# Second part's constants made beside the experts, zeros stored by ScalarE, first tiles planned first, last pair routed in three parts

## The chip, the cores and the metric

One core of one Trainium2 chip runs the whole program. The metric is the device time of one execution in microseconds (us). Three runs of the kernel before took 3497.92, 3501.64 and 3504.68 us, so the median is 3501.64 us.

## The reference, cut to what matters

The reference is a two-layer network over 16 sequences of 569 rows (441 image tokens and 128 text rows) of 256 numbers:

```python
h = tokenizer(x)                       # conv, one attention over the 441 tokens
h = concatenate([h, txt])              # 569 rows
h = h + window_attention(layernorm(h)) # 64-row windows
# experts: each row goes to the two best of 8, by gate probability
probs = softmax(layernorm(h) @ gate_w + gate_b)
top2_vals, top2_idx = top_k(probs, 2)
h = h + sum over the two experts e of
        probs[e] * (gelu(xf @ W1[e] + b1[e]) @ W2[e] + b2[e])
h = h + phasor_attention(layernorm(h))
h = h + lstm_layer(layernorm(h))       # 569 steps, hidden size 256, and sums over time
```

The change touches the seam between the window attention with its routing (the first part) and the experts, and the constants that only the phasor attention and the LSTM (the second part proper) need.

## The kernel before, in words

**First part (to L919).** The sequences are taken in 8 pairs. Each pair has 9 chunks of 128 rows. Nine streams of work (`features`, `norms`, `routing`, `texts`, `projections`, four slots of `windows`, two of `tokens`) are generators that announce their next instruction's engine and an estimate of its time. `Order.run` (L220) merges them into one written order by a list schedule, so PE, DVE, ACT and POOL run exactly the order that the planner wrote. SP, which only issues DMAs, is ordered by the framework's own scheduler. Inside a pair, `norms` and `windows` go through the chunks in the order `CHUNKS` = 7, 0, 1, 2, 3, 4, 5, 6, 8 (L362). Chunk 7 holds text only; chunks 6 and 8 need the last token unit. A finished window stores its rows in `HD` (L761) and hands them to `sent_rows`, which writes the normalised rows into `XN`.

**Routing (L767 to L891).** For each entry of `PARTS` (L364) the gate's logits, the softmax, the top two, and the rows' places in the experts' regions are computed. `place0` is the running first free place of each of the 8 experts; each part adds its counts to it (L864), so the parts form a chain. `send` then scatters each chunk's rows into `XS` in HBM by two indirect DMAs that POOL issues (L883), each followed by a small memset (L889). Pairs 0 to 6 are one part each; pair 7 has two: chunks 0 to 4 and chunks 5 to 8.

**Constants of the second part (L932 to L1027).** Between the two parts, in program order, stand the loads of `W_hh`, `lin`, `lstm_b`, `lb`, `W_ih`, `Wk1` and their like (ACT and SP issue them), DVE's work on `lin`, `lstm_b` and the bias pieces, POOL's memsets of `begins` and the four `X` buffers, and POOL's scalings of `W_hh` (L1006, six) and `W_ih` (L1013, two). The framework's scheduler mixes them with the end of the routing.

**Experts (L1035 to L1179).** `experts` turns the 8 counts into a table `where` for 79 tiles of 256 rows: which expert a tile belongs to and where its rows begin. The last tile of each expert can reach past its rows, so zeros are stored behind each expert's last row (L1112, eight stores of 256 KB issued by SP, each with an address that SP loads from `where` first). The rows' stores by `send` and the zeros are declared independent. SP issues four weight loads `w` (L1100, 1154 KB each), then the eight zero stores, then the row loads `xs` (L1106), which need everything in `XS` to have landed. The buffers of `w` lie where `XN` lay, so the first `w` load waits until the last `send` has landed. A tile is: transpose (L1140), copy (L1145), 8 matmuls (L1153), gelu (L1160), 8 matmuls (L1167), bias (L1173), store (L1174). Four slots interleave, and there are five buffers of `w` and `xs`.

Of the kernel before, what the change touches and what calls it, by code (L numbers as in the profile page):

```python
# [282 lines left out]
def kernel(ctx: ExitStack, tc: tile.TileContext, a: dict, out: bass.AP):  # L283
# [80 lines left out]
    PARTS = [(p, 0, NC) for p in range(NP - 1)] + [(NP - 1, 0, 5), (NP - 1, 5, NC)]  # L364
    WINDOWS = 4
    ROWS, XNS = 18, 4
    xns = {}

# [251 lines left out]
    def norms():  # L620

        for n in range(NC * NP):
            p, i = divmod(n, NC)
            c = CHUNKS[i]
            if n >= XNS:
                before = n - XNS
                yield "at", ("turned", before // NC, CHUNKS[before % NC])
            yield "at", ("token", p, min(c, 6)) if c != 7 else ("text", p)
            xn = xns[p, c] = wk.tile([128, D], F32, name=f"wxn{p}_{c}", tag="wxn", bufs=XNS)
            yield from norm(H[p, c], xn, f"w{p}_{c}", "w")  # L630
            first.mark(("columns", p, c))
# [20 lines left out]
    def windows(slot):  # L652

        kb, vb = KB[slot], VB[slot]
        for n in range(slot, NC * NP, WINDOWS):
            p, i = divmod(n, NC)
            c = CHUNKS[i]
# [104 lines left out]
            if n >= WINDOWS:  # L762
                before = n - WINDOWS
                yield "at", ("normed", before // NC, CHUNKS[before % NC])
# [169 lines left out]
    Whh = load_kxn(ls, "W_hh", 2, 4 * D, nc.scalar)  # L934
# [4 lines left out]
    nc.scalar.dma_start(lin, a["W_lin"].rearrange("(k p) n -> p k n", p=128))  # L939
    nc.vector.tensor_tensor(lin[:, :, :1], lin[:, :, 1:], lin[:, :, :1], ALU.subtract)  # L940
    nc.vector.tensor_copy(wl, lin[:, :, :1].to_broadcast([128, 2, 128]))
    shut = ls.tile([128, 1], F32, name="shut")
    nc.vector.tensor_tensor(shut, frow("b_lin", 1), frow("b_lin", 1, 1), ALU.subtract)
    nc.vector.tensor_scalar(shut, shut, 2.0, None, ALU.mult)
# [3 lines left out]
    by_unit = [cols[:, COL[n] : COL[n] + 2] for n in ("fw", "bw")]  # L948
    nc.vector.tensor_tensor(weights[:, 0, :], by_unit[0], by_unit[1], ALU.subtract)
    nc.vector.tensor_scalar(weights[:, 0, :], weights[:, 0, :], 0.5, None, ALU.mult)  # L950
    nc.vector.tensor_scalar(weights[:, 1, :], by_unit[1], -0.5, None, ALU.mult)
    nc.vector.tensor_scalar(weights[:, 2, :], by_unit[1], 0.5, None, ALU.mult)

    begins = {n: ls.tile([128, NB * (n + 1)], F32, name=f"begins{n}") for n in {n for _, _, n in RUNS}}
    for n, t in begins.items():
        nc.gpsimd.memset(t, 1.0)
        nc.gpsimd.memset(t.rearrange("p (b t) -> p b t", b=NB)[:, :, :1], 0.0)
# [6 lines left out]
    for t in XS_OF:  # L964
        nc.gpsimd.memset(t.rearrange("p k t x -> p (k t x)"), 0.0)
    one3 = ls.tile([128, 128], BF16, name="one3")
    nc.vector.memset(one3, 1.0)
# [3 lines left out]
    for t in bias3.values():  # L971
        nc.vector.memset(t, 0.0)
    with tc.tile_pool(name="lb", bufs=1) as lbp:
        lb = lbp.tile([128, 4 * D], F32, name="lb")
        for t, of in ((lstm_b, 0), (lb, 1)):
            nc.scalar.dma_start(t, a["lstm_b"][of].to_broadcast([128, 4 * D]))
        nc.vector.tensor_tensor(lstm_b, lstm_b, lb, ALU.add)
        v = lstm_b.rearrange("p (q r) -> p q r", r=128)[:, :, 64:96]
        nc.vector.tensor_scalar(v, v, 2.0, None, ALU.mult)

        def in_pieces(x, name):

            m = x.shape[0]
            pieces = lbp.tile([m, 3, D], BF16, name=name + "_pieces")
            left = lbp.tile([m, D], F32, name=name + "_left")
# [4 lines left out]
            return pieces  # L990

        for n, t in bias3.items():
            pieces = in_pieces(frow(n)[:1], n)
            for i in range(3):
                for j in range(2):
                    nc.sync.dma_start(t[i : i + 1, j, :], pieces[:, i, :])
# [3 lines left out]
    def gate_columns(w, gate):  # L1000
        return w.rearrange("p (q r) -> p q r", r=128)[:, :, 32 * gate : 32 * gate + 32]

    for k in range(2):
        for gate in (0, 1, 3):
            v = gate_columns(Whh[:, k, :], gate)
            nc.gpsimd.tensor_scalar(v, v, 0.5, None, ALU.mult)  # L1006

    bg = ExitStack()
    l1w = bg.enter_context(tc.tile_pool(name="l1w", bufs=1))
    Wih = load_kxn(l1w, "W_ih", 2, 4 * D)  # L1010
    for v in (Wih[:, 0, :], Wih[:, 1, :]):
        v = gate_columns(v, 2)
        nc.gpsimd.tensor_scalar(v, v, 2.0, None, ALU.mult)  # L1013
    l1 = {}
    for n in ("Wk1", "Wq1", "Wv", "Wo"):
        l1[n] = load_kxn(l1w, n, 2, D)
    for n in ("Wk2", "Wq2"):
        t = l1w.tile([128, 2, 2, 64], F32, name=n)
        for i in range(2):
            nc.sync.dma_start(t[:, :, i, :], a[n].rearrange("(k p) n -> p k n", p=128))  # L1020
        l1[n] = t
    masks = l1w.tile([128, 2, 128], F32, name="masks")
    nc.sync.dma_start(masks, a["masks"].rearrange("p (i n) -> p i n", i=2))
    none = l1w.tile([128, 1], F32, name="none")
    nc.vector.memset(none, 0.0)
    S = [l1w.tile([128, 2, 2, D], F32, name=f"S{p}") for p in range(0, NP, 2)]
    yat = l1w.tile([128, NP, 2, NC], mybir.dt.int32, name="yat")  # L1027
# [7 lines left out]
    def experts(g, mo, slots):  # L1035


        NT, most = TILES[g], E * REGION[g]
        count = tiling.tile([128, E], F32, name=f"count{g}", tag="count", bufs=1)
        nc.vector.tensor_tensor(  # L1040
            count, place0[:, g, :], frow("region", E, g * E), ALU.subtract
        )
        need = tiling.tile([128, E], F32, name=f"need{g}", tag="need", bufs=1)
# [5 lines left out]
        for e in range(E):  # L1049
            nc.vector.tensor_tensor(  # L1050
                end[:, e + 1 : e + 2], end[:, e : e + 1], need[:, e : e + 1], ALU.add
            )
        past = tiling.tile([128, NT, E], F32, name=f"past{g}", tag="past", bufs=1)
        nc.vector.tensor_tensor(
            past, frow("tile_no", NT).unsqueeze(2).to_broadcast([128, NT, E]),
            end[:, 1:].unsqueeze(1).to_broadcast([128, NT, E]), ALU.is_ge,
        )
        expert = tiling.tile([128, NT], F32, name=f"expert{g}", tag="expert", bufs=1)
        nc.vector.tensor_reduce(expert, past, AX.X, ALU.add)
        nc.vector.tensor_tensor(  # L1060
            past, past, need.unsqueeze(1).to_broadcast([128, NT, E]), ALU.mult
        )
        first = tiling.tile([128, NT], F32, name=f"first{g}", tag="first", bufs=1)
        nc.vector.tensor_reduce(first, past, AX.X, ALU.add)
        nc.vector.tensor_tensor(first, frow("tile_no", NT), first, ALU.subtract)
        nc.vector.tensor_scalar(first, first, float(TILE), None, ALU.mult)
        nc.vector.scalar_tensor_tensor(
            first, expert, float(REGION[g]), first, ALU.mult, ALU.add
        )
        where = tiling.tile([128, 2 * NT + E], mybir.dt.int32, name=f"where{g}", tag="where", bufs=1)  # L1070
        nc.vector.tensor_scalar(where[:, :NT], first, float(most), None, ALU.min)
# [867 lines left out]
```

## Time and profile before

| what | us |
|---|---|
| median of three runs | 3501.64 |
| the profiled execution | 3500.74 |
| its span, first to last instruction | 3498.9 |
| PE busy in the span | 3160.7 |
| DVE busy | 1958.2 |
| ACT busy | 1229.8 |
| POOL busy | 767.2 |

The profile is of one execution. The span is cut into 40 slices of 87.5 us; a digit tells how busy an engine was in a slice, in tenths. A windows view gives the busy time of each engine in any stretch, and a timeline lists the instructions of a stretch: start, duration, engine, line, operation, what it writes and reads, and how long the engine sat idle before, with what released it. "SPq" and "ACTq" are the sequencers that issue DMAs; their durations are issue times, not transfers.

### The profile page before, as it was taken

The page shows a single profiled execution, that of the slowest core. Times are in us where ns is not written, and L with a number is a line of the kernel's source. Part 1 is how long each engine was busy: PE and PEld are TensorE (multiplying, and loading weights), DVE is VectorE, ACT ScalarE, POOL GpSimd, SP SyncE. Part 2 cuts the span into 40 slices and gives each one's busy share as a digit, 9 for nine tenths or more (in the row PEclk, how much of TensorE's full clock was granted, in tenths as well). Part 3 has the DMA queues.
Part 4 walks back from the last instruction along what each step waited for, and adds up shares of the span by engine and source line. Part 5 has one row for each costly group of instructions (what it writes and reads, how often), then busy time and mean ns, then how long its engine had stood idle before and what let it go on. Part 6 is the DMA issues. An engine that isn't in the chain of part 4 may idle for free.

```text
span 3498.9 us, 91880 instructions
## 1 busy us (share of the span) xinstructions
PE 3160.7 (90%) x37356; PEld 2388.9 (68%) x37356; DVE 1958.2 (56%) x6420; ACT 1229.8 (35%) x3914; POOL 767.2 (22%) x1343
## 2 busy tenths in 40 slices
PE   6999999899659999996799999999999999999873
PEld 4666666666448888885677777777777777776542
DVE  4677677776621111113466666666676666666444
ACT  3555455544212222222433333333333333322220
POOL 1253455435610000003412111111112221001000
PEclk9999999999779999998999999999999999999996
DMA  4121222101266666662323222232232222231304
GB/s 172 51 68 42 74 82 80 37 22 39 97 229 231 223 230 223 228 215 75 110 63 90 82 85 79 84 86 83 78 86 80 73 77 79 69 107 60 127 29 108
DMA packets 186903, 363.17 MB, mean 104 GB/s; under 512 B 25600, under 2 KB 120880, under 8 KB 173424
## 3 DMA queue, kind: packets, MB, share of 16 engines
q1 hardware_dynamic: 164448, 310.04, 28.1%
q0 software_dynamic: 13824, 37.77, 3.4%
q10 hardware_dynamic: 8208, 9.48, 0.9%
q8 instruction: 295, 4.83, 0.6%
q14 instruction: 128, 1.05, 0.1%
HBM read 238.87 MB, written 118.33 MB: 102 GB/s over the span
## 4 chain that ended last, share of the span: by engine, by line
PE 43%; DVE 5%; ACT 3%; POOL 2%; issue 1%; DMA 1%; DVEq 0%; SPq 0%; ACTq 0%; POOLq 0%
PE g L1637 16%; PE xm_False L1503 7%; PE g L1602 3%; PE eq L1297 2%; PE z L1328 2%; PE ek L1297 2%; PE v L1317 2%; PE po_False L1473 2%; PE ds_False L1378 1%; PE fin L1700 1%; ACT act L1653 1%; DVE ab L1659 1%; PE r_False L1446 1%; ACT th L1678 1%; DVE cT L1672 1%
## 5 line engine op out<-in xcount | busy, mean ns | idle before, releaser
L1637 PE MATMUL g<-W_hh,X 128*16 128x128 f32 (+1 forms) x18176 | 606.6, 274 | 70.0 <-DVE X L1680 68.7
L1637 PEld LDWEIGHTS g<-W_hh,X 128*16 128x16 f32 (+1 forms) x18176 | 454.2, 103 | 242.6 <-DVE X L1680 194.1
L1653 ACT ACTIVATE act<-g 128x96 f32<-128x96 f32 x568 | 142.5, 251 | 658.2 <-PE g L1637 656.8
L1659 DVE SCALAR_TENSOR_TENSOR ab<-act 128x64 f32<-128x64 f32 x568 | 127.7, 225 | 383.9 <-ACT act L1653 379.3
L1167 PE MATMUL y<-w,hT 128*128 128x256 f32 x1264 | 289.9, 382 | 6.3 <-ACT hT L1160 2.5
L1269 POOL DMA_INDIRECT yg<-YS,yat x144 | 147.8, 1026 | 662.5 <-DMA YS<-ys 626.0
L1160 ACT ACTIVATE hT<-hp,w 128x256 f32<-128x256 f32 x316 | 132.5, 472 | 456.2 <-PE hp L1153 293.3
L1153 PE MATMUL hp<-xt,w 128*128 128x256 f32 x1264 | 285.7, 379 | 0.0
L1503 PE MATMUL xm_False<-W_ih,dxT_False 128*128 128x256 f32 x1088 | 282.0, 393 | 1.7 <-ACT dxT_False L1189 1.1
L1167 PEld LDWEIGHTS y<-w,hT 128*128 128x128 f32 x1264 | 236.7, 190 | 46.8 <-ACT hT L1160 16.1
L1153 PEld LDWEIGHTS hp<-xt,w 128*128 128x128 f32 x1264 | 238.8, 190 | 33.9
L1678 ACT ACTIVATE th<-cT 128x32 f32<-128x32 f32 x569 | 130.4, 229 | 371.7 <-DVE toT L1675 367.5
L1173 DVE TENSOR_TENSOR ys<-y,w 128x512 f32<-128x512 f32 x79 | 54.6, 691 | 357.9 <-PE y L1167 357.9
L1602 PE MATMUL g<-xp,ident 128*32 128x128 f32 x4552 | 231.0, 275 | 8.3 <-DMA xp<-XPD 8.3
L1503 PEld LDWEIGHTS xm_False<-W_ih,dxT_False 128*128 128x128 f32 x1088 | 193.4, 190 | 51.2 <-issue 26.6
L1212 POOL TENSOR_SCALAR r_False_rstd<-r_False_mv,cols 128x2 f32<-128x2 f32 x36 | 14.4, 400 | 785.5 <-DVE r_False_mv L1207 785.1
L1680 DVE SCALAR_TENSOR_TENSOR X<-toT,th 128x32 f32<-128x32 f32 x569 | 109.1, 192 | 116.6 <-ACT th L1678 114.8
L883 POOL DMA_INDIRECT XS<-XN,at x144 | 150.5, 1045 | 38.8 <-issue 24.6
L674 PE MATMUL wqk<-wxT,wqkv 128*128 128x128 f32 x1152 | 152.0, 280 | 6.2 <-ACT wxT L668 5.9
L674 PEld LDWEIGHTS wqk<-wxT,wqkv 128*128 128x128 f32 x1152 | 141.6, 194 | 21.8 <-ACT wxT L668 12.2
L1602 PEld LDWEIGHTS g<-xp,ident 128*32 128x32 f32 x4552 | 128.7, 110 | 38.9 <-issue 29.5
L1145 DVE COPY xt<-xtr 128x512 f32<-128x512 f32 x79 | 51.0, 686 | 159.0 <-PE xtr L1140 159.0
(341 smaller groups left out, 6022.0 us busy)
## 6 DMA issues: line engine op xcount, KB each, us to landing
w<-in_wpack SPq DMA_DIRECT2D x79, 1154.0 KB
xp<-XPD SPq DMA_DIRECT2D x71, 512.0 KB
XPD<-xp_False SPq DMA_DIRECT2D x256, 128.0 KB
taps<-in_taps SPq DMA_DIRECT2D x16, 1764.0 KB
xs<-XS SPq DMA_DIRECT2D x79, 256.0 KB
YS<-ys SPq DMA_DIRECT2D x79, 256.0 KB
HD<-h SPq DMA_DIRECT2D x72, 128.0 KB
fh<-HD SPq DMA_DIRECT2D x72, 128.0 KB
```

The source lines that it names most:

```text
L674: nc.tensor.matmul(qk[:, j, m, :], wqkv[:, k, D * j + 128 * m : D * j + 128 * m + 128], xT[:, k, :], start=(k == 0), stop=(k == 1),)
L883: fill(0, nc.gpsimd.indirect_dma_start(out=XS[0], out_offset=bass.IndirectOffsetOnAxis(ap=at[:, i, c - lo : c - lo + 1], axis=0), in_=XN[p ...
L1153: nc.tensor.matmul(hp[:, i, :], w1[:, k, hc * 128 : (hc + 1) * 128], xT[:, k, :], start=(k == 0), stop=(k == 1),)
L1167: nc.tensor.matmul(y[:, i, :], hT[:, hc, 128 * i : 128 * i + 128], w2[:, hc, :], start=(hc == 0), stop=(hc == 3),)
L1269: nc.gpsimd.indirect_dma_start(out=y, out_offset=None, in_=YS[g], in_offset=bass.IndirectOffsetOnAxis(ap=yat[:, p + j, i, c : c + 1], axis=0),
L1297: nc.tensor.matmul(e[:, oc, :], l1[f"W{name}1"][:, k, oc * 128 : (oc + 1) * 128], xT[:, k, :], start=(k == 0), stop=(k == 1),)
L1503: nc.tensor.matmul(mm[:, 256 * part : 256 * part + 256], xT[:, k, j * 128 : (j + 1) * 128], Wih[:, k, at_ : at_ + 256], start=(k == 0), st ...
L1602: nc.tensor.matmul(g[32 * q : 32 * q + 32, :128], ident[:, 32 * (t % 4) : 32 * (t % 4) + 32], xp[:, t // 4, 128 * q : 128 * q + 128], star ...
L1637: nc.tensor.matmul(g[32 * q : 32 * q + NB * (1 + half), :128], before[:, kk, NB * (1 - half) :], Whh[:, kk, 512 * half + 128 * q : 512 * h ...
L1653: nc.scalar.activation(act[:, :96], g[:, :96], AF.Tanh, scale=0.5)
L1659: nc.vector.scalar_tensor_tensor(ab, act[:, :64].rearrange("p (g x) -> p g x", g=2), 1.0, act[:, 64:].rearrange("p (g x) -> p g x", g=2), ...
L1678: nc.scalar.activation(th.rearrange("p k x -> p (k x)"), cT, AF.Tanh, scale=0.5)
```

## The change

1. `PARTS`: pair 7 is routed in three parts, chunks 0 to 3, 4 to 6, and 7 and 8. `unit(n)` gives the last pair the plain chunk order 0 to 8, so chunk 7's window comes eighth there instead of first.
2. The loads and preparations of the second part's constants go into a generator `prepare`, which the planner runs as a fifth stream beside the four slots of the experts. It asks for its loads after tile 1 and for most of its computing after tile 12. `W_hh`, `lin`, `lstm_b` and `lb` are now issued by SP; `lb` borrows a buffer of `S`.
3. The eight zero stores are issued by ACT from its own copy `behind` of `place0`, whose eight values are loaded at once. After each, ACT copies one column. A one-column gelu (`warm`) follows, which loads the gelu table.
4. The table `where` is computed for the first four tiles and then for the other 75. The running sum `end` is one scan instead of 8 additions.
5. SP loads the weights of two tiles ahead instead of four; tiles 2 and 3 load their rows first and then their weights.

```diff
-    PARTS = [(p, 0, NC) for p in range(NP - 1)] + [(NP - 1, 0, 5), (NP - 1, 5, NC)]
+    PARTS = [(p, 0, NC) for p in range(NP - 1)] + [(NP - 1, lo, hi) for lo, hi in ((0, 4), (4, 7), (7, NC))]
...
+    def unit(n):
+
+        p, i = divmod(n, NC)
+        return (p, CHUNKS[i]) if p < NP - 1 else (p, i)
...
-    Whh = load_kxn(ls, "W_hh", 2, 4 * D, nc.scalar)
+    Whh = ls.tile([128, 2, 4 * D], F32, name="W_hh")
...
+    def prepare(mo):
+
+        yield "at", ("tile", 0, 1)
...
+        lb = S[0].rearrange("p i k d -> p (i k d)")
+        nc.sync.dma_start(lin, kxn("W_lin"))
         for t, of in ((lstm_b, 0), (lb, 1)):
-            nc.scalar.dma_start(t, a["lstm_b"][of].to_broadcast([128, 4 * D]))
+            nc.sync.dma_start(t, a["lstm_b"][of].to_broadcast([128, 4 * D]))
+        nc.sync.dma_start(Whh, kxn("W_hh"))
+        nc.sync.dma_start(Wih, kxn("W_ih"))
+        for n in ("Wk1", "Wq1", "Wv", "Wo"):
+            nc.sync.dma_start(l1[n], kxn(n))
...
+        yield "at", ("tile", 0, 12)
+        yield "DVE", 0.2
+        nc.vector.tensor_tensor(shut, frow("b_lin", 1), frow("b_lin", 1, 1), ALU.subtract)
...
+        for k in range(2):
+            for gate in (0, 1, 3):
+                yield "POOL+", 0.85
+                v = gate_columns(Whh[:, k, :], gate)
+                nc.gpsimd.tensor_scalar(v, v, 0.5, None, ALU.mult)
+            yield "POOL+", 0.85
+            v = gate_columns(Wih[:, k, :], 2)
+            nc.gpsimd.tensor_scalar(v, v, 2.0, None, ALU.mult)
...
+        behind = tiling.tile([128, E], mybir.dt.int32, name=f"behind{g}", tag="behind", bufs=1)
+        nc.vector.tensor_copy(behind, place0[:, g, :])
+        _, at = nc.values_load_multi_w_load_instructions(
+            behind[0:1, :], engines=[mybir.EngineType.Activation], min_val=0, max_val=most - TILE,
+            skip_runtime_bounds_check_because=bounded,
+        )
+        between_ = tiling.tile([128, E], F32, name=f"between{g}", tag="between", bufs=1)
+        for e in range(E):
+            fill(g, nc.scalar.dma_start(
+                XS[g][bass.ds(at[e], TILE), :].rearrange("(i p) d -> p i d", p=128), zeros
+            ))
+
+            nc.scalar.copy(between_[:, e : e + 1], zeros[:, 0, :1])
...
+        warm = tiling.tile([128, 1], F32, name=f"warm{g}", tag="warm", bufs=1)
+        nc.scalar.activation(warm, count[:, :1], AF.Gelu)
+        plan.table = "gelu"
...
+        for lo, hi in ((0, slots), (slots, NT)):
+            n, no = hi - lo, frow("tile_no", hi - lo, lo)
+            past_, expert_, first_ = past[:, lo:hi], expert[:, lo:hi], first[:, lo:hi]
...
-        ahead = [weights(j) for j in range(slots)]
-        for e in range(E):
-            at = planned(2 * NT + e, most - TILE)
-            fill(g, nc.sync.dma_start(
-                XS[g][bass.ds(at, TILE), :].rearrange("(i p) d -> p i d", p=128), zeros
-            ))
-        for j, w in enumerate(ahead):
-            load(j, w)
+        ahead = [weights(j, e) for j, e in enumerate(planned(1, 0, 2, E - 1))]
+        for j in range(slots):
+            load(j, ahead[j] if j < 2 else None)
...
-            plan.run(experts(g, mo, 4))
+            plan.run(experts(g, mo, 4) + [prepare(mo)])
```

## The prediction

> **What bounds the kernel now.** I read the 40 slices of the span first: where PE is busy, nothing but less matrix work helps; where it is not, some chain of waits is.
>
> ```profile
> PE   6999999899659999996799999999999999999873
> POOL 1253455435610000003412111111112221001000
> PEclk9999999999779999998999999999999999999996
> GB/s 172 51 68 42 74 82 80 37 22 39 97 229 231 223 230 223 228 215 75 110 63 90 82 85 79 84 86 83 78 86 80 73 77 79 69 107 60 127 29 108
> ```
>
> PE is at 90% nearly everywhere. The dip that this change can reach is in the eleventh and twelfth slice, 875 to 1050 us, just ahead of the seven slices in which the experts stream weights. I cut that seam into its steps with a windows view (columns: stretch, its length, busy us and instructions of each engine, granted PE clock, DMA share, GB/s):
>
> ```profile
> 942.00:950.00 8.00, 1.75 (x19) 0.76 (x19) 4.34 (x24) 1.08 (x3) 6.86 (x13) 0.58 0.82 264
> 950.00:963.00 13.00, 1.03 (x4) 0.93 (x4) 9.60 (x34) 0.00 (x0) 12.36 (x24) 0.50 0.75 254
> 963.00:975.40 12.40, 0.00 (x0) 0.00 (x0) 11.33 (x43) 0.00 (x0) 10.91 (x19) 0.50 0.43 126
> 975.40:998.20 22.80, 0.00 (x0) 0.00 (x0) 0.43 (x2) 0.00 (x0) 0.04 (x1) 0.50 0.86 314
> 1002.00:1596.00 594.00, 587.73 (x2825) 509.54 (x2824) 103.00 (x155) 133.83 (x317) 0.00 (x0) 1.00 0.65 217
> ```
>
> PE does 2.8 us of work from 942 to 998. Then the experts run 594 us with PE 99% busy and DMA at 65%: what starts earlier there ends earlier. The timeline names the links of the chain:
>
> ```profile
> 949.51 0.16 DVE L940 TENSOR_TENSOR lin<-lin 128x2 f32<-128x2 f32 x1 [3.49 <-DMA lin<-in_W_lin]
> ...
> 954.86 1.23 DVE L977 TENSOR_TENSOR lstm_b<-lstm_b,lb 128x1024 f32<-128x1024 f32 x1 [1.75 <-DMA lb<-in_lstm_b]
> ...
> 956.12 2.42 DVE L979 TENSOR_SCALAR lstm_b<-lstm_b 128x256 f32<-128x256 f32 x1
> ...
> 958.46 4.98 POOL L1006 TENSOR_SCALAR W_hh<-W_hh 128x256 f32<-128x256 f32 x6
> ...
> 963.60 1.03 POOL L883 DMA_INDIRECT XS<-XN,at  x1 [0.15 <-DVE end L1050]
> ...
> 975.35 2.92 SPq L1100 DMA_DIRECT2D w<-in_wpack  x4
> 978.77 11.39 SPq L1112 DMA_DIRECT2D XS<-zeros  x8
> 995.26 4.24 SPq L1106 DMA_DIRECT2D xs<-XS  x5
> ...
> 998.23 3.17 PE L1140 MATMUL xtr<-ident,xs 128*128 128x128 f32 x12 [37.96 <-DMA xs<-XS]
> ```
>
> The chain: the last window's rows are added at 939.73; routing of the last part, in which DVE waits for `lin`, then for `lb`, and works on `lstm_b`, all of the second part; POOL scales `W_hh` before it sends; eight sends; the last lands and SP issues weights at 975.35; eight zero stores until 990.16; they land at 995.26; rows arrive at 998.2; the first expert matmul is at 1001.88.
>
> **The change, step by step.** The changed kernel's written order is known. After the first tiles it is the old one on PE, instruction for instruction, so all effects are in this seam and in the SP queue. It also shows that "beside the experts" holds in part: SP issues `lin`, `lstm_b`, `lb`, `W_hh`, `W_ih`, `Wk1` (3.4 MB) ahead of the first weight load, and POOL has the `begins` and `X` memsets and three of the `W_hh` scalings ahead of the last four sends.
>
> *Last window.* Chunk 7's window moves from first to eighth. Between the last token's rows and the last window's rows PE gets 167 matmul instructions instead of 146; 21 at about 0.27 us are 5.7 us, which leave the busy stretch before (PE 93% there) and enter one where it is busy 71% (898 to 942). So the last token comes about 5 us earlier and the tail is longer. By PE's queue, the last chunk's projections end about 24 us after the last token's rows (15.4 now), and the rest takes about 22 (24.4 now): +7. Net +1.5, bounds −4 and +7: rows added at 941.2.
>
> *Routing to the last `place0`.* Now 20.97 us (939.73 to 960.70). Chunks 4 to 6 from the gate bias to `place0`: about 26 DVE instructions, 6.2 us at the 0.2 to 0.42 us that such rows take, and 1.6 us through PE and back (959.1 to 960.7): 7.8. PE transposes chunks 7 and 8 only then; to the gate bias that is 4.4 (941.96 to 945.57, plus one more pair of transposes). Softmax to the running count: 945.57 to 953.1 takes 7.5 now, less 3.0 of the `lin` wait and 0.5 to 0.8 since two chunks are narrower than four: 4.1. PE and back 1.6. Sum 17.9: `place0` at 959.1. That is only 3 us shorter, though 5.4 (953.1 to 958.5) of `lb` waits and work fall out too: the extra part costs about 7.
>
> *Sends.* 1.9 us on (1.7 now), at 961.0, the rows' places are ready. POOL has by then six sends of chunks 4 to 6 (1.27 each), one `X` memset (0.98) and three scalings (0.83 each) behind it, ending near 961.8. Four sends instead of eight: the last starts at 961.8 + 3×1.27 = 965.6; SP's weight load came 2.6 after the last send's start (972.74 to 975.35): **968.2, 7.1 earlier**. If `W_hh` lands later than I think (2.1 MB after 946), the scalings wait, up to +5.
>
> *Zeros.* ACT starts at 959.5, about 1 us for the eight values, then 0.38 issue + 0.2 copy + 0.1 each: the last at 966, landed 968.7 to 971 (the 5.1 us of now, 990.16 to 995.26, had 4.7 MB of weights ahead of it). The sixth store waits for `W_ih` to have landed, near 963. The trace of before has no such store on ACT; the near row is SP's 1.42 us each, with its own address load. With 1.6 each the last lands near 977.
>
> Here a rule speaks against the change. The Trainium skill (DMA: Bandwidth & Descriptors, section Issuing engines are not separate DMA queues) says that issuing from another engine only saves the sequencer's time to initiate, "which is usually small relative to the DMA itself". The row says: the eight issues held SP 11.4 us, the bytes (2.1 MB at the 314 GB/s of that stretch) are 6.7 us. By the rule the zeros still share the transfers ahead of the first matmul: w0, w1, three xs and zeros are 5.2 MB, 16.7 us from 968.2. By the row the zeros move before the weights, since ACT need not wait for the sends: 3.15 MB, 10.0 us. I take the row; the rule is my main rival.
>
> *To the first matmul.* 968.2 + 10.0, and 1.5 for transposes and copy: 979.8 instead of 1001.88. Weights of tile 2 are due some 4 us later and arrive about then (4.3 MB, 13.8 us: 982); I take 1 us of stall.
>
> *At nothing.* The plan of the first tiles (some 15 DVE instructions, 3 us) ends near 962.5, under the wait for the sends, as the whole plan did before (`where` at 968.7, load at 975.35). The plan of the other 75 and the `yat` work, 4.8 + 7.0 us, end near 976 on DVE, 2 us before the first copy; without that cover up to 2 us. The gelu table (1.28 us, at 1003.92 now) loads under the transfers. `prepare`'s DVE and POOL work lies beside 594 us in which DVE is 17% busy. The constants left for SP then (1.2 MB) fit into 65% of the transfer time.
>
> *Sum*, against the profiled execution: 1001.9 − 979.8 − 1 = 21.1, and 3500.7 − 21 = 3479.7. That run is 0.9 under the median; I say **3480**.
>
> **The rivals.**
> 1. *Transfers decide the start*: the rule above, or `W_hh` late, or slow stores on ACT. For it: 254 to 314 GB/s in three of the four stretches of the seam, and 3.4 MB of constants still first. Against: at 963 to 975 only 126 GB/s. The start comes at 986 to 990: gain 12 to 16, **3487**.
> 2. *The tail gains too*: chunk 7's window fills idle PE, the last rows come 4 us earlier, and DVE's softmax is not held up by POOL's memsets: gain 26 to 30, **3473**. For it: PE busy 8.5 of the 14 us from 928 to 942. Against: +8 us of PE queue before the last projections.
> 3. *Slower: SP's queue.* Nine of `prepare`'s loads stand between `w` and `xs` in SP's in-order queue, and several wait for an earlier weight load to land before they issue. Weights are asked for about 25 us before use and land in 5, so 20 us are spare. If each of the nine held SP a tile's 7.5 us, 67 less 20 is lost: 3480 + 47, **3527**. It decides from about 41 us of holding (20 spare + 21 gained). Against: the DMAs waited for are issued a tile or more before.
> 4. *It doesn't do what it says*: the constants stay ahead, as the order shows for 3.4 MB; if POOL waits for `W_hh` until after 975, nothing is gained: **3500**.
>
> **How the numbers follow.** Forecast (gain 17 to 26) 0.52, rival 1 0.24, rival 2 0.14, rival 4 0.06, rival 3 0.04. No change is within 7 us (0.2%, what these runs can tell apart). Faster: 0.52 + 0.24 + 0.14 = 0.90; same 0.06; slower 0.04. The range takes the forecast's 3475 to 3484, rival 1 down to a gain of 10 and rival 2 up to 32: 3469 to 3491.
>
> **What would show it.** Right: no DVE wait for `lin` or `lb`; the last send's start near 966 and the first weight load near 968; zero stores from ACT between 960 and 967 about 0.7 us apart; the first expert matmul near 980; 594 us of experts after that. Wrong: zero stores that start when `W_ih` has landed and run past 970; POOL idle before a scaling of `W_hh`; PE idle on `w` in the first tiles; an expert stage over 597 us.

## The result, and the profile after

| | us | |
|---|---|---|
| before, median of 5 | 3501.46 | 3497.80 to 3504.68 |
| after, median of 5 | 3484.36 | 3482.21 to 3487.42 |
| ratio | 0.9955 | 95% interval 0.9942 to 0.9967 |

The change makes the kernel faster by 0.45% (15.8 us by the ratio, 17.1 by the medians). The profiled execution of the changed kernel is the slowest of its five: 3487.42 us, span 3485.6. Between the two profiled executions lie 13.3 us.

The slices of the changed kernel, the same rows as before:

```profile
PE   6999999899679999996899999999999999999873
PEclk8999999999889999998999999999999999999996
GB/s 173 51 64 43 77 82 80 36 24 37 92 266 226 227 225 235 223 194 88 97 68 89 78 86 81 78 87 87 81 81 84 75 75 77 72 105 60 127 29 108
```

PE's twelfth slice (958.6 to 1045.7) rose from 5 to 7, and the twelfth value of GB/s from 229 to 266: the experts' stream begins earlier in it. One other slice of PE differs, the twentieth, which rose from 7 to 8: the experts end in it, earlier than before. The seam by stretches (length, busy us and instructions of PE, PEld, DVE, ACT and POOL, granted PE clock, DMA share, GB/s):

```profile
950.00:959.00 9.00, 2.82 (x15) 1.67 (x13) 4.40 (x26) 1.06 (x3) 7.88 (x14) 0.50 1.00 384
959.00:970.00 11.00, 0.00 (x0) 0.00 (x0) 10.00 (x34) 3.01 (x10) 10.21 (x16) 0.50 0.83 289
970.00:980.00 10.00, 0.27 (x2) 0.30 (x3) 4.58 (x21) 0.00 (x0) 2.48 (x4) 0.50 0.93 343
985.00:1579.00 594.00, 588.18 (x2815) 509.50 (x2813) 108.48 (x176) 132.54 (x316) 0.00 (x0) 1.00 0.66 220
```

The experts fill 594 us as before. The stretch from the last send to the first transposes, 22.8 us long before, is gone. In its place DMA is busy nearly all the time from 950 on. The timeline gives the links of the chain:

```profile
949.34 2.75 POOL L1007 MEMSET X<- 128x1024 f32 x3
...
952.26 0.97 POOL L884 DMA_INDIRECT XS<-XN,at  x1 [0.16 <-issue]
...
958.82 1.76 DVE L1078 TENSOR_SCALAR need<-count 128x8 f32<-128x8 f32 x1
...
959.58 0.97 POOL L1007 MEMSET X<- 128x1024 f32 x1
...
960.62 2.55 POOL L1040 TENSOR_SCALAR W_hh<-W_hh 128x256 f32<-128x256 f32 x3
...
964.91 0.56 ACTq L1065 DMA_DIRECT2D XS<-zeros  x1
...
967.19 0.97 POOL L884 DMA_INDIRECT XS<-XN,at  x1 [0.19 <-issue]
...
969.76 0.92 SPq L1134 DMA_DIRECT2D w<-in_wpack  x2
...
979.73 2.79 PE L1169 MATMUL xtr<-ident,xs 128*128 128x128 f32 x12 [21.68 <-DMA xs<-XS]
...
984.24 0.47 PE L1169 MATMUL xtr<-ident,xs 128*128 128x128 f32 x1 [1.71 <-DMA xs<-XS]
...
984.50 9.46 PE L1182 MATMUL hp<-xt,w 128*128 128x256 f32 x30
```

The last send starts at 967.19, the first weight load is issued 2.57 later, and the first rows arrive at 979.7. Then comes a line that the prediction had not in its sum: PE waits 1.71 us more for one single transpose, and only behind it stands the first expert matmul. The zeros are all issued by 965.5. DVE waits for neither `lin` nor `lb`.

All runs below are told by their links, counted from the end of the last window's row addition (942.69 in this trace, 939.73 before), since what lies ahead of it differs between chips. "hp" is the first expert matmul, "y" the first of the second layer, and "end" the end of the experts' last matmul. The first load is one of weights, in `rows_first` one of rows. Each line is one profiled execution; that of `two_parts` is the fastest of its six, that of `after_again` the slowest of its fifteen.

| kernel (chip) | rows added | last send | first load | first transposes | first hp | y | end |
|---|---|---|---|---|---|---|---|
| before | 939.7 | +33.0 | +35.6 | +58.5 | +62.2 | +69.9 | +658.0 |
| after | 942.7 | +24.5 | +27.1 | +37.0 | +41.8 | +51.1 | +640.2 |
| consts_before (A) | 945.2 | +30.2 | +35.2 | +44.5 | +49.4 | +55.9 | +645.2 |
| zeros_sp (A) | 944.5 | +24.5 | +27.1 | +43.2 | +50.8 | +59.7 | +649.0 |
| rows_first (A) | 944.0 | +25.4 | +29.4 | +32.6 | +39.8 | +48.3 | +637.9 |
| hold (A) | 943.4 | +21.3 | +26.3 | +35.7 | +41.5 | +49.7 | +644.3 |
| late3 (B) | 952.3 | +24.5 | +27.1 | +36.5 | +39.1 | +47.1 | +636.1 |
| two_parts (B) | 937.6 | +28.3 | +30.9 | +40.7 | +45.0 | +51.5 | +640.8 |
| plan_whole (B) | 952.6 | +24.6 | +27.9 | +37.4 | +43.2 | +52.6 | +642.2 |
| warm (B) | 955.3 | +24.5 | +27.1 | +48.0 | +49.4 | +56.0 | +645.0 |
| after_again (C) | 954.7 | +24.5 | +27.1 | +36.5 | +41.8 | +50.1 | +639.2 |
| best2 (C) | 937.9 | +28.0 | +30.6 | +40.4 | +43.0 | +50.3 | +639.6 |
| best3 (C) | 938.5 | +28.3 | +30.9 | +37.2 | +39.0 | +46.5 | +635.8 |
| warm7 (C) | 953.1 | +24.5 | +27.1 | +36.6 | +41.2 | +49.1 | +638.6 |

The first set ran on a chip A, where the kernel before took 3500.6 us; the others on chips B and C, where it took 3582.9 and 3584.7. For the changed kernel 79 of the 90 us between its two traces (`after` and `after_again`) lie behind the experts. So across sets only ratios to the kernel before, and these links, are compared.

### The profile page after: what moved, and what is told of

The parts are those of the page before. It is cut to its first block, busy times and chain, and to the rows that moved or that the text cites. A ratio compares the mean times of both kernels' runs of the same rounds, so it can differ in the third digit from the quotient of the medians.

```text
span 3485.6 us, 91891 instructions
## 1 busy us (share of the span) xinstructions
PE 3162.5 (91%) x37343; PEld 2392.5 (69%) x37360; DVE 1959.2 (56%) x6443; ACT 1232.8 (35%) x3924; POOL 765.2 (22%) x1343
## 4 chain that ended last, share of the span: by engine, by line
PE 43%; DVE 5%; ACT 3%; POOL 2%; issue 1%; DMA 0%; DVEq 0%; SPq 0%; ACTq 0%; POOLq 0%
PE g L1666 16%; PE xm_False L1532 7%; PE g L1631 3%; PE eq L1326 2%; PE z L1357 2%; PE ek L1326 2%; PE v L1346 2%; PE po_False L1502 2%; PE ds_False L1407 1%; PE fin L1729 1%; ACT act L1682 1%; DVE ab L1688 1%; PE r_False L1475 1%; ACT th L1707 1%; DVE cT L1701 1%
## 5 line engine op out<-in xcount | busy, mean ns | idle before, releaser
L1196 PEld LDWEIGHTS y<-w,hT 128*128 128x128 f32 x1264 | 236.7, 190 | 46.6 <-ACT hT L1189 15.8
L884 POOL DMA_INDIRECT XS<-XN,at x144 | 150.2, 1043 | 44.9 <-issue 24.5
L1701 DVE STREAM_TRANSPOSE cT<-act 128x32 f32<-128x32 f32 x569 | 120.4, 212 | 19.3
```

Of the source, the lines that this page charges most:

```text
L884: fill(0, nc.gpsimd.indirect_dma_start(out=XS[0], out_offset=bass.IndirectOffsetOnAxis(ap=at[:, i, c - lo : c - lo + 1], axis=0), in_=XN[p ...
L1196: nc.tensor.matmul(y[:, i, :], hT[:, hc, 128 * i : 128 * i + 128], w2[:, hc, :], start=(hc == 0), stop=(hc == 3),)
L1701: nc.vector.transpose(cT, act[:, 96:])
```

## The experiments

### Two parts of the change undone: the zeros and the constants

`zeros_sp` issues the zero stores from SP again.

```diff
-        _, at = nc.values_load_multi_w_load_instructions(behind[0:1, :], engines=[Activation], ...)
-            fill(g, nc.scalar.dma_start(XS[g][bass.ds(at[e], TILE), :]..., zeros))
...
         ahead = [weights(j, e) for j, e in enumerate(planned(1, 0, 2, E - 1))]
+        for e in range(E):
+            at = nc.values_load(behind[0:1, e : e + 1], engines=[SP], ...)
+            fill(g, nc.sync.dma_start(XS[g][bass.ds(at, TILE), :]..., zeros))
```

> The changed kernel with the eight zero stores back on SP (three of them fall ahead of the first weights, five between weights 1 and rows 0). By the row of the profile before (1.42 us of SP per store): five stores hold SP 7 us, and the rows wait for the last to land, time 3491 to 3494. By the rule that issuing from another engine only saves the initiation, which is small: within 2 us of 3484.

Measured: 3493.86 us, ratio 0.9979 (0.9971 to 0.9988); 9.5 us over the changed kernel by the medians. The timeline of `zeros_sp`, SP's sequencer:

```profile
971.56 0.94 SPq L1123 DMA_DIRECT2D w<-in_wpack  x2
973.01 3.95 SPq L1138 DMA_DIRECT2D XS<-zeros  x5
...
983.94 1.30 SPq L1129 DMA_DIRECT2D xs<-XS  x2
```

The size is what the row foretold, but not for its reason. The five stores hold SP 4 us, 0.8 each and not 1.42. They are issued by 977, and the row loads then wait until 983.94 for the last to land, behind 2.3 MB of weights. Of the 10.9 us by which the rows are asked for later, about 4 are issuing and 7 are landing. By the rule that the prediction weighed (the Trainium skill, DMA: Bandwidth & Descriptors, section Issuing engines are not separate DMA queues: another engine saves only the time to initiate) the move would be worth the 4 us of issuing. The measured 10.9 is more, because the move also changes the order of the bytes: ACT may store while SP has to wait for the sends, so the zeros move ahead of the weights.

`consts_before` puts the constants back where they were made (the block of the kernel before, no `prepare`).

```diff
-    Whh = ls.tile([128, 2, 4 * D], F32, name="W_hh")
+    Whh = load_kxn(ls, "W_hh", 2, 4 * D, nc.scalar)
...
-            plan.run(experts(g, mo, 4) + [prepare(mo)])
+            plan.run(experts(g, mo, 4))
```

> The changed kernel with the second part's constants made where the kernel before made them (loads on ScalarE's and SP's queues, work ahead of the plan, no prepare), the other three edits kept. T1: VectorE waits again for lin (3.0 to 3.5 us) and lb, works 4 us on lstm_b within the routing of the last part, and GpSimd scales W_hh six times ahead of the sends: the start comes 8 us later, time 3492. T2 (only the bytes count, and most of them are ahead of the weights in both): 1.2 MB more ahead of the weights are 3 to 4 us, time 3488.

Measured: 3491.57 us, ratio 0.9971 (0.9960 to 0.9981); 7.2 over the changed kernel. The link that moves is the last send, from +24.5 to +30.2, and with it the first load, by 8.1; the first matmul comes 7.6 later and the end 5.0. The end loses less because PE is already at full clock at its first expert matmul here (the 30 matmuls up to "y" take 6.50 us, in the changed kernel 9.30; see below). T1 has its number, but only in part by its reasons. The last `place0` comes 21.4 us after the rows instead of 15.8, which is the whole delay of the sends. But VectorE does not wait for `lin`, and `lstm_b` takes 1.6 us, not 4. What holds it are a small cast beside POOL's `X` memsets, the other work on the bias pieces, and a wait for one of them to land:

```profile
951.80 3.46 DVE L987 CAST l_bv_pieces<-flow 1x256 bf16<-1x256 f32 x1
...
952.37 2.74 POOL L966 MEMSET X<- 128x1024 f32 x3
...
964.50 0.17 DVE L843 TENSOR_TENSOR picked<-both,picked 128x16 f32<-128x16 f32 x1 [1.66 <-DMA l_bo<-l_bo_pieces]
```

The first weight load then comes 5.1 us behind the start of the last send instead of 2.6; that part was not traced further.

### What the first matmul waits for

`rows_first` changes only the order in which SP asks.

```diff
-        ahead = [weights(j, e) for j, e in enumerate(planned(1, 0, 2, E - 1))]
-        for j in range(slots):
-            load(j, ahead[j] if j < 2 else None)
+        xs = [rows(0)]
+        ws = [weights(0)]
+        xs += [rows(j) for j in range(1, slots)]
+        ws += [weights(j) for j in range(1, slots)]
```

> The changed kernel with another order of its first loads on SP: rows 0, weights 0, rows 1 to 3, then weights 1 to 3 (weights 0, weights 1, rows 0, 1, 2, weights 2, rows 3 before). T1 with order as the mis-sized term (rows 2 wait for weights 0 to land, rows 3 come behind 2.4 MB and stand ahead of the first matmul on PE): rows 0 and weights 0 land first, the first matmul comes near 978 to 980 instead of 984.5, tile 1's weights are then up to 2 us late, time 3480. T2 (bytes): tile 0 starts earlier and waits for tile 1's weights as long as before, time 3484 within 1.5.

Measured: 3482.69 us, ratio 0.9946 (0.9933 to 0.9960): 1.7 us under the changed kernel by medians, inside the intervals. From the first load (of rows) to the first matmul it takes 10.4 us; from the first load (of weights) it took 14.7 in the changed kernel, so the order does count. But SP now asks for five more constants ahead of the first row load, which comes 2.3 later. The test is not clean.

`late3` moves one transpose in PE's written order: tile 3's stream pauses longer, and its first transpose falls behind the first two tiles' matmuls.

```diff
-                    yield "pause", 5.0
+                    yield "pause", 5.0 if j < 3 else 9.0
```

> The changed kernel with one thing moved in the written order of PE: the first transpose of tile 3 no longer stands ahead of the first expert matmul, but behind the first two tiles' matmuls. T1 (the mis-sized term of the sum is that transpose: its rows come behind the weights of tile 2, 1.2 MB at 400 GB/s, and PE waits 1.71 us idle for them): the first matmul comes right behind the twelve transposes, near 982.5 instead of 984.5[...]; time 3481 to 3482. T2 (transfers alone decide): PE waits as long for weights 1 or 2 afterwards, time 3484 within 1.

Measured: 3569.29 us, ratio 0.9964 (0.9951 to 0.9977), against 3571.39 and 0.9970 (0.9961 to 0.9979) for the changed kernel on chip C. The total cannot tell it apart; the links can. The timeline of `late3`:

```profile
988.82 2.79 PE L1169 MATMUL xtr<-ident,xs 128*128 128x128 f32 x12 [21.16 <-DMA xs<-XS]
...
991.40 8.18 PE L1182 MATMUL hp<-xt,w 128*128 128x256 f32 x30
```

The first matmul follows the transposes without a wait, 12.0 us after the first weight load (14.7 in the changed kernel), and the experts end at +636.1 instead of +640.2 or +639.2. By these links T1 holds: 2.7 us at the first matmul. The rest at the end is the clock, which here was raised 3 us into the 30 matmuls (they took 8.02 us).

`hold` keeps the constants truly out of the seam: SP's order in the second part is the written one, and POOL's scalings come first in `prepare`, so that they wait for `W_hh`.

```diff
-    with tc.manual_schedule(engines=ENGINES):
+    with tc.manual_schedule(engines=ENGINES | {mybir.EngineType.SP}):
         mo = tc.alloc_tile_pool(name="moe", bufs=1)
```

> The changed kernel (3484.4 us) with the constants kept out of the seam: SP's loads of them are queued behind the third expert tile's own loads, and on GpSimd all their work stands behind the last sends. Theory T1 (the start is a chain: last sends, first weight load, rows, first matmul): the last four sends are no longer behind the X memset (0.97) and three W_hh scalings (2.55), and VectorE's 1.76 us row beside that memset shortens, so the first weight load is issued about 3 us earlier (near 966.7), the first matmul as much, time 3481. Theory T2 (the bytes in flight set the start: DMA share 1.00 at 950 to 959 and about 1.0 at 980 to 985, of which 3.4 MB are the constants): 3.4 MB at 350 GB/s are 9.7 us less, first matmul near 975 to 977, time 3476. Theory T3 (the prediction's slower rival, SP's queue): the fourteen constant loads now stand behind one another with 4.6 MB between two expert tiles, PE waits for w of a tile around the seventh, time over 3486.

Measured: 3496.43 us, ratio 0.9987 (0.9979 to 0.9996), 12 us over the changed kernel. Timeline and two-microsecond stretches of `hold`:

```profile
964.69 1.02 POOL L884 DMA_INDIRECT XS<-XN,at  x1 [0.19 <-DMA XS<-zeros]
...
969.62 0.90 SPq L1134 DMA_DIRECT2D w<-in_wpack  x2
...
1033.53 1.09 PE L1169 MATMUL xtr<-ident,xs 128*128 128x128 f32 x4 [4.19 <-DMA xs<-XS]
```

```profile
962.00:964.00 2.00, 0.00 (x0) 0.00 (x0) 1.86 (x6) 0.57 (x3) 1.66 (x3) 0.50 1.02 346
964.00:966.00 2.00, 0.00 (x0) 0.00 (x0) 1.90 (x5) 0.38 (x2) 1.63 (x4) 0.50 1.00 342
966.00:968.00 2.00, 0.00 (x0) 0.00 (x0) 1.71 (x9) 1.68 (x3) 0.00 (x0) 0.50 1.02 334
```

The last send starts 3.2 earlier, as T1 said, yet the first load only 0.8: the zeros, issued from 960.5 on, fill DMA to 968 at some 340 GB/s, and the last sends land among them. T2's 9.7 us do not come either: with 3.4 MB less in the seam the first matmul comes 0.3 earlier. T3's mechanism does come, at a place of its own: fourteen loads stand together between tiles, SP needs 16 us for them (1006.5 to 1022.1), and PE waits at 1033 (it is busy 6.47 of the ten us from 1030). The experts end 4.1 later against the rows added, and 4.2 more are lost behind them, where SP also follows the written order; that second loss was not traced further.

### The granted clock

`warm` puts 18 pairs of matmuls with unused results on PE between the plan and the first transposes.

```diff
+        hot = ps.tile([128, 512], F32, name=f"hot{g}", tag="bank3", bufs=1)
+        for _ in range(WARM):
+            nc.tensor.matmul(hot[:, :E], ident, first[:, :E], start=True, stop=True)
+            nc.tensor.matmul(hot, ident, flow[:, :512], start=True, stop=True)
```

> The changed kernel with 18 pairs of matmuls (128x8 and 128x512) put on PE between the plan and the first transposes; their results are not used. They begin when VectorE has the plan (about 968) and end near 980. T1 (part of the loss is the granted clock: it is 0.50 from 984.5 to 990.2, where the kernel before had 1.00 from its first matmul on): PE is at full clock at the first expert matmul, which is worth half of 5.7 us, time 3481.5. T2 (PE only waits the longer for weights that arrive at 400 GB/s): 3484 within 1. If the pairs end after the rows arrive, up to 2 us slower.

Measured: 3576.89 us, ratio 0.9984 (0.9976 to 0.9993). The pairs were dearer than thought (1.08 us each at full clock) and overran the rows' arrival by about 11 us. But from the first expert matmul to the first of the second layer, 30 matmuls, it took 6.57 us instead of 9.30 (8.36 in `after_again`, the same kernel). In the changed kernel the stretches behind 984 read:

```profile
984.00:986.00 2.00, 1.76 (x5) 1.50 (x6) 0.00 (x0) 0.00 (x0) 0.00 (x0) 0.50 0.97 396
986.00:988.00 2.00, 2.00 (x6) 1.55 (x6) 0.00 (x0) 0.00 (x0) 0.00 (x0) 0.50 1.08 428
988.00:990.00 2.00, 2.00 (x6) 1.60 (x5) 0.00 (x0) 0.84 (x2) 0.00 (x0) 0.50 0.97 383
990.00:992.00 2.00, 2.00 (x10) 1.74 (x9) 0.00 (x0) 0.00 (x0) 0.00 (x0) 0.95 0.84 271
```

PE counts as fully busy in them and does 6 matmuls in two microseconds where it later does 10 or 11: the clock is 0.50 until about 990.2. In the kernel before the same rows are

```profile
1000.00:1002.00 2.00, 1.70 (x9) 1.18 (x8) 1.30 (x3) 0.00 (x0) 0.00 (x0) 0.66 0.90 266
1002.00:1004.00 2.00, 2.00 (x11) 1.77 (x10) 0.13 (x1) 0.08 (x1) 0.00 (x0) 1.00 0.86 324
```

with full clock from about 1001.4 on, just ahead of the first expert matmul at 1001.88.

Why the same work meets the clock so differently can be worked out from the traces. The granted clock is 0.50 or 1.00 there, so a mean in between gives the moment of the step. Three half-microseconds of the changed kernel:

```profile
942.00:942.50 0.50, 0.39 (x2) 0.00 (x0) 0.23 (x1) 0.00 (x0) 0.35 (x2) 0.58 0.00 0
945.50:946.00 0.50, 0.00 (x0) 0.00 (x0) 0.47 (x2) 0.00 (x0) 0.41 (x2) 0.83 0.00 0
990.00:990.50 0.50, 0.50 (x3) 0.42 (x2) 0.00 (x0) 0.00 (x0) 0.00 (x0) 0.80 1.07 354
```

The steps are at 942.42 (up), 945.83 (down) and 990.20 (up): 3.41 us apart, and 13 times 3.41. Worked out in the same way, all steps between 880 and 1020 us in each of the fourteen traces of this case lie on such a grid of 3.41 us, whose points fall differently in each trace. So the busy time has to be read between points of the grid, first in the changed kernel, then in `two_parts`, with the line of its wait:

```profile
979.96:983.37 3.41, 2.56 (x12) 2.16 (x11) 2.07 (x3) 0.00 (x0) 0.00 (x0) 0.50 1.03 409
983.37:986.79 3.42, 2.55 (x7) 2.11 (x8) 0.00 (x0) 0.00 (x0) 0.00 (x0) 0.50 1.02 408
986.79:990.20 3.41, 3.41 (x10) 2.69 (x9) 0.00 (x0) 0.84 (x2) 0.00 (x0) 0.50 0.98 389
```

```profile
978.26:981.67 3.41, 2.79 (x12) 2.38 (x12) 1.97 (x3) 0.00 (x0) 0.00 (x0) 0.50 1.03 411
```

```profile
982.45 0.33 PE L1169 MATMUL xtr<-ident,xs 128*128 128x128 f32 x1 [1.40 <-DMA xs<-XS]
```

In `two_parts` (as in `consts_before`, and in `hold`, which lost the clock again in a longer wait) the twelve transposes, 2.79 us, lie between two points, and the clock is up at the second, during the same wait for tile 3's rows. In the changed kernel the wait lies across a point, leaves 2.56 and 2.55 us of work on either side, and the clock comes only behind the third stretch. How much work a stretch needs is not settled: 3.40 us of unused matmuls in one stretch of `warm` (from 980.40) did not raise it.

`warm7` is `warm` with `WARM = 7`.

> The changed kernel with 7 pairs of unused matmuls on PE (18 of them ran 10 us past the arrival of the rows, but the first 30 expert matmuls then took 6.73 us where the changed kernel took 9.46). T1 (clock): the pairs end near the rows' arrival, the first expert matmul comes when it came, and its stretch takes 6.7 us: 2.7 us under the changed kernel. T2 (the weights of tiles 1 and 2 are the bound in that stretch): within 1 us of the changed kernel.

Measured: 3571.72 us, ratio 0.9970 (0.9960 to 0.9980), the same as the changed kernel beside it (3571.39). The clock was up from 983.6 on and down again at 993.8, in the wait for tile 3's rows, 2.88 us long just ahead of the first expert matmul; the 30 matmuls took 7.94 us. Neither theory is settled by its total. The numbers for these 30 matmuls, 6.50 (`consts_before` and `two_parts`), 6.57 (`warm`), 7.94, and 8.36 to 9.30 for the changed kernel, show that the clock is worth up to 2.8 us here and that a short wait can take it back.

### The other two parts undone, and the best versions

`two_parts`:

```diff
-    PARTS = ... + [(NP - 1, lo, hi) for lo, hi in ((0, 4), (4, 7), (7, NC))]
+    PARTS = ... + [(NP - 1, 0, 5), (NP - 1, 5, NC)]
...
-        return (p, CHUNKS[i]) if p < NP - 1 else (p, i)
+        return p, CHUNKS[i]
```

> The changed kernel with the last pair routed in two parts again, in the window order of the kernel before (edit 1 undone, the others kept). By the prediction's own sums the third part costs about 7 us of routing and tail (place0 comes 5.3 to 6.8 us earlier without it) and saves four sends of 1.27 behind the last places (5.1 us): T1 says the first weight load comes 0 to 1.7 us earlier, time 3483 to 3484.5. T2 (the sends are the chain, and the part's own routing hides under the sends of the part before): the load comes 3 to 5 us later, time 3487 to 3489.

Measured: 3561.98 us, ratio 0.9949 (0.9931 to 0.9967). Its median is below that of every three-part kernel on chips B and C, though its interval overlaps those of most of them. Behind the added rows nothing is won or lost: the last send is 3.8 later with two parts and the experts end at +640.8 against +640.2 and +639.2, the clock helping. The difference lies ahead: the last rows are added at 937.6 instead of 952 to 955.

`plan_whole`:

```diff
-        for lo, hi in ((0, slots), (slots, NT)):
+        for lo, hi in ((0, NT),):
```

> The changed kernel with the table of tiles planned in one piece (edit 4's split undone; the scan instead of eight adds stays). Two more 0.25 MB loads of constants fall ahead of the first weights in SP's order. T1: the plan of all 79 tiles takes 4.8 us more on VectorE and ends near 968, still ahead of the last send's landing at 969.7, so nothing is lost by it: 3484 to 3486. T2 (the plan is on the path): 4 to 5 us slower, 3489.

Measured: 3572.36 us, ratio 0.9973 (0.9964 to 0.9983) against 0.9970 for the changed kernel on chip C. The first load comes 0.8 later. The totals do not tell the two apart; by the links the split is worth a microsecond or two at most, and two more loads of constants are in that.

`after_again` is the changed kernel as a reference on chip C; `best2` is `two_parts` and `late3` together; `best3` adds the load order w0, xs0 to xs2, w1, xs3, w2, w3, and five pairs of unused matmuls that begin behind POOL's last send.

> The changed kernel itself, as the reference for the three that follow on the same chip. All theories: 0.9955 of the time before, within the interval 0.9942 to 0.9967 measured first.

Measured: 3571.39 us, ratio 0.9970 (0.9961 to 0.9979): a smaller gain than on the first chip.

> The changed kernel with the last pair in two parts and the first transpose of tile 3 behind the first two tiles' matmuls. T1: the transpose is worth the 4.1 us that it gave from the last rows to the experts' end, and the third part is worth nothing (from the last rows to the experts' end 640.8 us with two parts, 640.2 with three, while the last rows come no later with two): 4 to 6 us under the changed kernel, more if the last rows come earlier. T2 (three parts help by the sends they save): 1 to 4 us over the kernel with the moved transpose alone, so 0 to 3 us under the changed kernel.

Measured: 3560.45 us, ratio 0.9938 (0.9923 to 0.9954), 10.9 us under the changed kernel. T1 had 4 to 6, and more if the last rows came earlier; they came 16.8 earlier. From the first load to the first matmul it takes 12.4 us, in `two_parts` 14.2: the moved transpose again.

> As the last one, with the first loads in the order weights 0, rows 0 to 2, weights 1, rows 3, weights 2 and 3, and with five pairs of unused matmuls on PE behind GpSimd's last send, which raise the granted clock before the first transposes. T1: 1.2 MB less ahead of the first matmul are 2 to 3 us, and full clock at the first tile 1.6 us: 3 to 5 us under the last one. T2 (order and clock only move the wait to tile 1's or 2's weights): within 1 us of the last one.

Measured: 3559.85 us, ratio 0.9938 (0.9923 to 0.9953), not told apart from `best2` by the total, though its links are 4 us shorter (end +635.8). Both beat both kernels. Part of why the last rows come so late with three parts on chip C shows in ten-microsecond stretches, first of `after_again`, then of `best2`:

```profile
810.00:820.00 10.00, 6.64 (x76) 4.67 (x74) 2.06 (x6) 3.30 (x10) 7.21 (x14) 0.97 0.24 94
820.00:830.00 10.00, 9.51 (x42) 7.41 (x44) 1.85 (x6) 2.05 (x7) 2.81 (x5) 0.69 0.07 26
```

```profile
810.00:820.00 10.00, 7.58 (x42) 5.86 (x40) 1.71 (x6) 2.25 (x7) 6.40 (x13) 1.00 0.20 80
820.00:830.00 10.00, 9.48 (x85) 6.10 (x83) 7.52 (x15) 6.64 (x19) 4.00 (x5) 1.00 0.05 16
```

In `after_again` PE stands still 3.85 us in this stretch and then works at a clock of 0.69: 42 matmuls where `best2` does 85. ScalarE waits 5.5 us there for something outside the core's own records; in `best2` ScalarE has such a wait too (4.9 us) and PE keeps its clock. Of the 16.8 us between the last rows of these two traces, 5.1 are there already at the 59th of the 72 row additions (797.3 against 792.2), 4.7 come until the 63rd, around this wait, and 7.0 in the last nine, as many as a pair has. In the traces of `before`, `after` and chip A no such wait is recorded, and the last rows of `after` came 3.0 later with three parts, not 17. So a cost of edit 1 ahead of the seam is shown, but its size belongs to the chip, and what ScalarE waited for stays open.

## Why the prediction was right, step by step

The forecast was 3480 with a gain of 21 us; measured are 15.8 by the ratio and 17.1 by the medians, at the edge between the forecast's gain (17 to 26) and that of the first rival (12 to 16). So the number alone cannot tell the two apart; the links can. The mechanism is the forecast's: the waits for `lin` and `lb` and the zeros leave the chain, and what starts earlier ends earlier. The first rival's reasons did not come: `W_hh` had landed in time, ACT issued a store every 0.6 to 1.2 us, the zeros were out of the way of the weights, and in `hold` 3.4 MB less in the seam did not bring the first matmul forward by more than 0.3.

| step (span of the profiled execution) | predicted | measured |
|---|---|---|
| last rows added | 941.2 | 942.7 |
| from there to `place0` | 17.9 | 15.8 |
| from `place0` to the rows' places | 1.9 | 3.1 |
| last send starts | 965.6 | 967.2 |
| first weight load | 968.2 | 969.8 |
| from there to the first transposes | 10.0 | 10.0 |
| from there to the first expert matmul | 1.5 | 4.8 |
| lost in the first tiles | 1 | 2.5 |
| earlier at the experts' end | 21.1 | 14.8 |

Of the missing 6.3 us, three terms account for all.

- **Last sends, 1.6 us.** The tail was 1.5 worse than the taken value and routing 2.1 better; that these two cancel is luck. What made the sends late is POOL: the rows' places were ready at 961.5 and POOL's three scalings of `W_hh` ran until 963.2. The prediction had POOL free at 961.8. Its sum for POOL has six sends, one memset and three scalings; it left out that three more `X` memsets stood ahead of the six sends, until 952.1, while those sends' places were ready at 950.3. DVE's `need` row took 1.76 us beside POOL's memset of `X`, and with the row behind it the places took 3.1 us from `place0` instead of 1.9; here that hid behind POOL. In `hold`, without the memsets and scalings, the two rows took 0.17 and 0.19 and the last send came 3.2 earlier.
- **Transposes to matmul, 3.3 us.** The 10.0 us from the load to the transposes came as forecast, though with DMA at 334 GB/s and not 314. The term "1.5 for transposes and copy" was mis-sized. Tile 3's first transpose stands ahead of the first expert matmul in PE's written order, and its rows stand behind tile 2's weights in SP's. Moving this one transpose (`late3`) brings 12.0 us from first load to first matmul, 0.5 more than the 11.5 predicted.
- **First tiles, 1.5 us.** One microsecond of stall on weights was allowed; no such wait came. What came was half clock, 9.30 us for 30 matmuls that take 6.5 at full clock; the prediction has no term for the clock. The kernel before had its step up just ahead of its first expert matmul. A rule stands behind the grid of 3.41 us: the Trainium skill (TensorE: Matmul & The Clock Gate, Part 1: The HAM clock gate) says that the clock is raised after a busy window of about 3.4 us of a free-running counter. The grid agrees with it. That such a window must be busy throughout does not: 2.79 us of work in 3.41 were enough in three traces, and the measurement decides. So this term is in part chance: `after_again`, the same kernel, took 8.36.

From the experts' end to the end of the span the profiled execution lost 1.5 us more; the other executions of the changed kernel have spans of 3480.4 to 3483.6, so that is within their spread.

Where cost was put at nothing, it was nothing: the plan of the other tiles ended under the sends, `prepare` beside the experts cost them nothing (594 us), and the third rival, SP's queue, did not come in the changed kernel. `hold` shows how near it was: the same loads in one block cost PE a wait. Six of the constants' loads still stand ahead of the first weights, which looked like a fault of the change; by `hold`, it seems rather to keep them out of that queue.

The second rival's premise, that chunk 7's window ahead of the last rows is a gain, is refuted: with three parts the rows came later on every chip, by 3.0 us in the changed kernel's first profile (3.7 to 5.5 in the four kernels on chip A) and by 14 to 18 on B and C. Edit 1 pays back 3.8 us at the sends. On chip A that is about even by these links, though two parts were not timed there; on B and C it is a loss, by the medians of `two_parts` and `best2` (the latter clear of the changed kernel's interval, with the moved transpose in it). So what the change gains comes from edits 2 and 3, whose undoing costs 7.2 and 9.5 of the 17.1 us, with the split plan a microsecond or two. Edit 5, two weight loads ahead instead of four, was not undone alone, so its share is open.

## What to carry to other kernels

Follow a start-up chain to the first instruction that stands **in the engine's order**, not to the first whose data are there: one transpose of a later tile, put ahead by a planner that does not know when its rows land, put the first expert matmul off by 2.7 us. Moving a store to another queue pays by what it may overtake (7 us here) more than by the issue time it saves (4 us). And undo each part of a change alone: here one of five worked against the others on two of three chips, and the total hid it.

## What the runs showed of the hardware that was not expected

- Between 880 and 1020 us the granted clock steps only at points of a grid of 3.41 us, in each of the fourteen traces. Where these points fall decides whether the same 30 matmuls take 6.5 or 9.3 us; the same kernel twice took 9.30 and 8.36. A wait of 2.88 us just ahead of them was enough to lose a clock that unused matmuls had raised.
- A small DVE operation (8 columns) took 1.76 us beside a 0.97 us POOL memset of 1024 columns, and 0.17 without it. In `consts_before` a cast of 256 columns took 3.46 beside a run of such memsets, and its like 0.27 behind them: it ended only when the run of memsets did.
- Eight zero stores held SP 11.4 us before, 0.8 us each in `zeros_sp`, and 0.38 to 1.03 each on ACT. Why the issue times differ was not found.
- Three chips ran the kernel before in 3500.6, 3582.9 and 3584.7 us. On the slower two, ScalarE has waits of up to 10.8 us for something outside the core's records, 49 to 63 us in all behind the experts, which the traces of `before`, `after` and chip A do not have. What they are was not found.
